# Attention quotients: reciprocals of all 512 columns of a group, in place of one column in 32 of turned squares

## The chip, the cores and the metric

The kernel runs on one core of one Trainium2 chip. The metric is the device time of one execution in microseconds. The engines are named as in the profile: PE (matmuls) with PEld (its weight loads), DVE (vector engine), ACT (scalar engine), POOL (GpSimd) and SP (which issues nearly all DMAs).

## The reference

A transformer block with adaptive layer norm. x is (8, 1024, 512) and the condition (8, 512), all fp32. The rows of the condition give six vectors per batch row (shift, gain and gate for attention and for the MLP).

```python
mod = jax.nn.silu(condition) @ Wada + bada
sh_a, sc_a, gt_a, sh_m, sc_m, gt_m = jnp.split(mod, 6, axis=1)
xm = (layernorm(x) * g1 + be1) * (1.0 + sc_a[:, None, :]) + sh_a[:, None, :]
x = x + gt_a[:, None, :] * attention(xm, Wqkv, Wproj, bproj)   # 16 heads of 32, causal softmax
xm = (layernorm(x) * g2 + be2) * (1.0 + sc_m[:, None, :]) + sh_m[:, None, :]
h = gelu(xm @ W1 + b1)                                          # 512 -> 2048, exact gelu
x = x + gt_m[:, None, :] * (h @ W2 + b2)
```

The place of interest is the division in the softmax: the weighed values of a head and a query are divided by the sum of that query's exponentials.

## The kernel before

**Blocks and groups.** The 8 x 1024 tokens are cut into 16 blocks of 512 tokens (`blocks`, `NB` = 16), two to a batch row. The 16 heads are cut into 4 groups of 4 (`NC` = 4, `HPG` = 4), since 4 heads of 32 channels fill 128 partitions. So there are 64 pairs of block n and group g. For each pair PE computes the scores twice: once row by row for the maxima (`scores`, tile `sc`, L1679), which DVE masks (L1691) and reduces (`mx`, L1694), and once transposed with the maxima subtracted (`weights_T`, tile `st`, L1758 and L1770). ACT exponentiates the latter into `pT` (L1782), POOL zeroes what lies above the diagonal (L1787) and adds the tiles of exponentials up (L1911). PE multiplies `pT` with the values into `po` (L1810). `sc` and `st` share one buffer of four PSUM banks.

**The end of a group.** `finish` has PE add up the exponentials over the keys by a product with a tile of ones (L1831). With 32 equal columns of ones for each head, each of a head's 32 partitions holds the same sum of a query: in the bank, a square of 32 partitions by 32 columns has 32 different sums, each repeated down a column. ACT copies the bank to `rec` (L1840) and `po` to `top` (L1843); both tiles have one buffer. Then DVE works in pieces. `gather(i)` transposes a quarter of `rec` in squares of 32x32 into `squares` (L1850), so that the sums of a square stand in one column, one to a partition, and takes the reciprocal of that one column in 32, four columns for a quarter (L1852, into `inverse`). `spread_out` transposes `inverse`, each column repeated 32 times, back over `rec` (L1857). The quotient, `top` times `rec`, is written into the block's query tile `qT`, which is free by then: by POOL (L1885) in 61 of the 64 groups, and by DVE in the last group of block 0 (`first_end`, L1874), the last but one of block 15 (L1882) and the last of all (L1866, in quarters).

**The projection and the rest.** `qT` then goes through Wproj (`project_out`; for the odd blocks, but the last, `project_quarters`), the second layer norm and the MLP. The linear layers use a Strassen-like scheme on halves of 256 (`strassen`, products of 16 matmuls on L217, evacuated by DVE at L208 and L194 or by ACT at L197 and L204). Block n's attention runs beside the linear layers of its neighbours, as `plan` lists them.

**What sets the order.** The order on each engine is written out when the program is built. `now` holds a clock for each engine; `note` adds the booked duration of an instruction to it and keeps when each tile is written and left. `step_aside`, `work` and `pace` choose with these clocks what PE does next (attention, or a step of the linear layers), and `sooner` and `either` choose the engine of some operations. DVE's work at the end of a group is handed to `add_job`; `run_jobs` puts jobs on DVE where its booked clock is not ahead of PE's, those of a block's last group ahead of others. For `first_end` and for the very last group the work is issued at once. So a booked duration that changes can move instructions of every engine. The bookings of the operations concerned are `160 + 1.05 * wide + 100` (`wide` = 128) for `gather`, `140 + 1.05 * m` (m = 512, or 128 at the very end) for `spread_out`, and 1285 for POOL's quotient.

**Loads.** SP issues the loads of weights into a ring of 8 buffers (`fetch`), of x, and of scratch copies in DRAM, in one queue. From block 2 on (two blocks at the end excepted) x is normalized, transposed in squares on DVE (L704), written to DRAM (L713) and read back turned (L718, `hat_a`), before gain and shift are applied (L775 on DVE, L781 on ACT) and sums for the products are formed (L791, L793). Two steps `gates` multiply the condition with parts of Wada (L524). In the opening `scores_by_heads` (L1649, L1666) takes a unit of scores head by head through the three banks of the linear layers where these are free.

Of the kernel before, what the change touches and what calls it, by code (L numbers as in the profile page):

```python
# [9 lines left out]
F32 = mybir.dt.float32  # L10
# [12 lines left out]
def kernel(  # L23
# [33 lines left out]
    nc = tc.nc  # L57
    B, T, D = x.shape
    HD = W1.shape[1]
    P = 128  # L60
    hd = D // H
    scale = float(hd) ** -0.5
    TB = 512
    NTT = TB // P
    NHALF = T // TB
    NC = D // P
# [15 lines left out]
    small = ctx.enter_context(tc.tile_pool(name="small", bufs=2))  # L82
# [22 lines left out]
    def due(reads=(), writes=()):  # L105
        t = 0.0
        for k in reads:
            t = max(t, written.get(k, 0.0))
        for k in writes:
            t = max(t, left.get(k, 0.0))  # L110
        return t

    def note(engine, ns, reads=(), writes=(), port=False):
        start = max(now[engine], due(reads, writes))
        if port:
            start = max([start] + [b for a, b in pool_spans if a <= start < b])
        end = start + ns
        now[engine] = end
        if engine == "POOL":
            pool_spans.append((start, end))  # L120
            del pool_spans[:-16]
        for k in reads:
            left[k] = max(left.get(k, 0.0), end + SYNC)
        for k in writes:
            written[k] = end + SYNC
        return end
# [9 lines left out]
    def note_pe(ns, form, reads=(), writes=()):  # L136
        now["PE"] = max(now["PE"], due(reads, writes))
        if shape[0] != form:
            shape[0] = form
            now["PE"] += SWITCH  # L140
        note("PE", ns, reads)
        spent[0] += ns
        for k in writes:
            written[k] = now["PE"] + PIPE

    def note_act(ns, func, reads=(), writes=()):
        if func is not None and table[0] != func:
            table[0] = func
            ns += TABLE
        note("ACT", ns, reads, writes)  # L150
# [31 lines left out]
    def lin_bank():  # L182
        i = min(
            (i for i in range(3) if not live[i]),
            key=lambda i: left.get(("l", i), 0.0),
        )
        live[i] = True
        return i
# [54 lines left out]
    def mlp_steps(n):  # L243
        return [("u", n, i) for i in range(NQ)] + [("d", n, part) for part in range(4)]
# [9 lines left out]
    for w in range(1, NB):  # L254
        n = w - 1
        m = mlp_steps(n)
# [29 lines left out]
    n = NB - 1  # L286
# [115 lines left out]
    Q = P // NTT  # L402
# [81 lines left out]
    def spread(o):  # L484
        return cols[:, o : o + NC].unsqueeze(2).to_broadcast([P, NC, B])

    def norm_columns(name, shift_at, gain_at, o_g, o_b):

        gain = const.tile([P, NC, B], F32, tag=f"gain{name}", name=f"gain{name}")
        shift = const.tile([P, NC, B], F32, tag=f"shift{name}", name=f"shift{name}")  # L490
        one_plus = small.tile([P, NC, B], F32, tag="onep", name=f"onep{name}", bufs=1)
        nc.vector.tensor_scalar(one_plus, modT[:, ts(gain_at, NC), :], 1.0, None, ALU.add)
        nc.vector.tensor_tensor(gain, one_plus, spread(o_g), ALU.mult)
        nc.vector.tensor_tensor(shift, one_plus, spread(o_b), ALU.mult)
        nc.vector.tensor_tensor(shift, shift, modT[:, ts(shift_at, NC), :], ALU.add)
        return gain, shift
# [60 lines left out]
    def add_job(job, reads, first=False):  # L557

        at = sum(1 for other in jobs if other[2]) if first else len(jobs)
        jobs.insert(at, (job, reads, first))  # L560

    def run_jobs(everything=False):
        while jobs and (
            everything or (now["DVE"] <= now["PE"] and due(jobs[0][1]) <= now["PE"])
        ):
            jobs.pop(0)[0]()
# [854 lines left out]
    def perform(step):  # L1421
        kind = step[0]
        if kind == "mod":
            yield from modulation(step[1])
        elif kind == "norm_columns_a":
            columns_of["a"] = norm_columns("a", 0, 1, O_G1, O_BE1)
        elif kind == "gates":
            yield from gates(step[1])
# [112 lines left out]
    def step_aside(reads, writes):  # L1541


        while threads():
            if linear_wait() == NEVER:
                hurry()
            own, other = wait_of((reads, writes)), linear_wait()
            if done_linear[0] < stream["due"]:
                if other > own + 100:
                    break  # L1550
            elif own <= max(other, 50):
                break
            work()
        while BANK in writes and bank_at() == NEVER:
            work()
        run_jobs()
        run_act_jobs()
        run_pool_jobs()
        run_preparation()
# [260 lines left out]
    def finish(n, g):  # L1820

        run_jobs(True)
        acc, slot = totals.pop((n, g))
        more = unadded if (n, g) == first_end else []
        step_aside([("acc", n, g), *(("p", slot) for *_, slot in more)], [BANK])
        bank = lin_bank()
        terms = [(0, TB, acc, slot)] + [(c0, w, pT, slot) for parts, pT, slot in more for _, c0, w, _ in parts]
        for i, (c0, w, term, held) in enumerate(terms):
            for j in range(HPG):
                r = slice(j * hd, (j + 1) * hd)  # L1830
                nc.tensor.matmul(  # L1831
                    banks[bank][r, TB - w :], ones, term[:, j, c0 : c0 + w],
                    start=i == 0, stop=i == len(terms) - 1, skip_group_check=True,
                )
            note_pe(2 * COLUMN * w, "columns", [("acc", n, g), ("p", held)], [("l", bank)])
        free_p.extend([slot, *(held for *_, held in more)])
        top = tmp.tile([P, TB], F32, tag="top", name=f"top_{n}_{g}", bufs=1)
        rec = tmp.tile([P, TB], F32, tag="rec", name=f"rec_{n}_{g}", bufs=1)
        kr = "rec"
        nc.scalar.copy(rec, banks[bank])  # L1840
        note_act(585, None, [("l", bank)], [kr])
        live[bank] = False
        nc.scalar.copy(top, outs.pop((n, g)))  # L1843
        note_act(585, None, ["po"], ["top"])
        part = TB // 4
        wide = TB // 4

        def gather(i):
            squares = small.tile([P, wide], F32, tag="squares", name=f"squares_{n}_{g}_{i}", bufs=1)
            nc.vector.transpose(squares, rec[:, ts(i, wide)])  # L1850
            some = inverse[:, ts(i, wide // Q)]
            nc.vector.reciprocal(some, squares.rearrange("p (a i) -> p a i", i=Q)[:, :, 0])  # L1852
            note("DVE", 160 + 1.05 * wide + 100, [kr], [kr])

        def spread_out(i=0, m=TB):
            some = inverse[:, i * m // Q : (i + 1) * m // Q].unsqueeze(2).to_broadcast([P, m // Q, Q])
            nc.vector.transpose(rec[:, ts(i, m)].rearrange("p (a i) -> p a i", i=Q), some)  # L1857
            note("DVE", 140 + 1.05 * m, [kr], [kr])

        inverse = small.tile([P, TB // Q], F32, tag="inverse", name=f"inverse_{n}_{g}", bufs=1)  # L1860
        if (n, g) == groups[-1]:
            for i in range(NTT):
                gather(i)
                spread_out(i, part)
                some = slice(i * part, (i + 1) * part)
                nc.vector.tensor_tensor(qTs[n][:, g, some], top[:, some], rec[:, some], ALU.mult)  # L1866
                note("DVE", 200, [kr, "top"], [("att", n, i)])
            return

        if (n, g) == first_end:  # L1870
            for i in range(4):
                gather(i)
            spread_out()
            nc.vector.tensor_tensor(qTs[n][:, g, :], top, rec, ALU.mult)  # L1874
            note("DVE", 700, [kr, "top"], [("att", n)], port=True)
            written["attended", n] = 0.0
            return

        def quotient():
            spread_out()  # L1880
            if n == NB - 1 and g == NC - 2:
                nc.vector.tensor_tensor(qTs[n][:, g, :], top, rec, ALU.mult)  # L1882
                note("DVE", 700, [kr, "top"], [("att", n)], port=True)
            else:
                nc.gpsimd.tensor_tensor(qTs[n][:, g, :], top, rec, ALU.mult)  # L1885
                note("POOL", 1285, [kr, "top"], [("att", n)])
            if g == NC - 1:
                written["attended", n] = 0.0

        for i in range(4):  # L1890
            add_job(lambda i=i: gather(i), [kr], g == NC - 1)
        add_job(quotient, [kr], g == NC - 1)

    shared = {}
# [194 lines left out]
```

## Time and profile before

| | |
|---|---|
| median of 3 runs | 3508.98 us (3507.87 to 3513.93) |
| the profiled execution | 3501.11 us, span 3499.4 us |
| granted TensorE clock | 0.998 of full speed, mean |
| busy: PE, DVE, POOL, ACT | 98%, 63%, 60%, 35% of the span |
| instructions: PE, DVE, POOL, ACT | 55101, 2808, 2255, 1272 |

Busy times add up over an engine's instructions. In rows of instructions the engine stands first, then what is written, what is read and the shapes. A time in square brackets is how long the engine was idle ahead of the row, and for whom. An fp32 matmul has two records in the trace.

### The profile page before, as it was taken

The numbers are of one execution on the slowest core, as the hardware profiler recorded it, in microseconds if no ns is written. First come the engines' busy times: TensorE is split into PE (matmuls) and PEld (weight loads), VectorE is DVE, ScalarE is ACT, GpSimd is POOL, SyncE is SP. The second block draws the span as 40 slices with busy tenths as digits, with TensorE's granted clock in tenths as the row PEclk, the third lists the DMA queues.
The fourth block names the chain that finished last, engine by engine and source line by source line (L and its number), as shares of the span: only waits on it lengthen the run. The fifth ranks groups of instructions, "written<-read, shape, count | busy, mean of one in ns | idle before, by whom it ended". The sixth has DMA issues, their size and how long they took to land. (4 is left out here: it accounts for less than half of the span.)

```text
span 3499.4 us, 122173 instructions
## 1 busy us (share of the span) xinstructions
PE 3441.3 (98%) x55101; PEld 1750.9 (50%) x55101; DVE 2203.8 (63%) x2808; ACT 1212.8 (35%) x1272; POOL 2113.7 (60%) x2255
## 2 busy tenths in 40 slices
PE   8999999999999999999999999999999999999999
PEld 4444455445544555445554455544555445554555
DVE  5775675565666566565666656665666656656573
ACT  2335333342343513335232442333423333323521
POOL 3667847667366663767627676375762857628640
PEclk9999999999999999999999999999999999999999
DMA  6763444535535455363554535545455454543344
GB/s 213 237 188 104 137 125 139 147 104 171 147 118 158 119 162 149 103 182 116 152 152 127 159 116 152 153 137 146 130 154 143 130 144 132 154 126 98 104 134 140
DMA packets 335580, 498.84 MB, mean 143 GB/s; under 512 B 27724, under 2 KB 184460, under 8 KB 331476
## 3 DMA queue, kind: packets, MB, share of 16 engines
q1 hardware_dynamic: 334944, 490.99, 47.8%
q8 instruction: 434, 7.11, 0.8%
q14 instruction: 86, 0.70, 0.1%
q10 hardware_dynamic: 116, 0.03, 0.0%
HBM read 432.13 MB, written 56.69 MB: 140 GB/s over the span
## 5 line engine op out<-in xcount | busy, mean ns | idle before, releaser
L1911 POOL TENSOR_TENSOR pT<-pT,pT 128x256 f32<-128x256 f32 (+3 forms) x1254 | 1224.7, 1012 | 238.9 <-PE po L1810 123.9
L1782 ACT ACTIVATE pT<-st 128x2048 f32<-128x2048 f32 x288 | 541.1, 1879 | 1017.5 <-PE st L1770 886.3
L217 PE MATMUL bank<-w,hT 128*32 128x256 f32 x14336 | 822.1, 380 | 0.0
L1694 DVE TENSOR_REDUCE mx<-sc 128x4 f32<-128x2048 f32 (+3 forms) x383 | 663.3, 1753 | 200.5 <-PE sc L1679 194.7
L217 PEld LDWEIGHTS bank<-w,hT 128*32 128x32 f32 x14336 | 448.0, 110 | 389.8 <-issue 109.7
L217 PE MATMUL bank<-xm_m,w 128*32 128x256 f32 x8192 | 497.4, 381 | 2.3 <-ACT p_u L197 1.0
L217 PE MATMUL bank<-t_m,w 128*32 128x256 f32 x6144 | 384.0, 380 | 2.5 <-DVE qT L208 1.4
L217 PEld LDWEIGHTS bank<-xm_m,w 128*32 128x32 f32 x8192 | 255.5, 110 | 227.3 <-issue 56.6
L1787 POOL TENSOR_SCALAR_AFFINE_SELECT pT<-pT 128x512 f32<-128x512 f32 x256 | 177.3, 710 | 313.7 <-ACT pT L1782 313.3
L1679 PE MATMUL sc<-kT,qT 32*128 32x512 f32 (+3 forms) x3064 | 328.0, 520 | 3.1 <-DVE mx L1694 1.8
L1691 DVE TENSOR_TENSOR sc<-sc,mask 128x1024 f32<-128x1024 f32 (+1 forms) x160 | 162.8, 1017 | 255.2 <-PE sc L1679 210.8
L1810 PE MATMUL po<-pT,v 128*32 128x512 f32 (+3 forms) x3048 | 301.7, 490 | 2.5 <-POOL pT L1787 2.3
L1770 PE MATMUL st<-qT,kT 32*128 32x512 f32 (+3 forms) x3072 | 302.7, 487 | 0.0
L217 PEld LDWEIGHTS bank<-t_m,w 128*32 128x32 f32 x6144 | 188.9, 110 | 178.8 <-issue 49.8
L217 PE MATMUL bank<-xm_a,w 128*32 128x256 f32 x3968 | 241.6, 380 | 2.4 <-ACT p_k L197 1.1
L1679 PEld LDWEIGHTS sc<-kT,qT 32*128 32x128 f32 x3064 | 129.2, 183 | 182.4 <-issue 82.4
L208 DVE TENSOR_TENSOR hT<-bank,u_u 128x512 f32<-128x512 f32 x186 | 126.0, 686 | 127.2 <-PE bank L217 126.5
L217 PE MATMUL bank<-t_a,w 128*32 128x256 f32 x2944 | 182.3, 380 | 1.4 <-ACT qT L204 0.9
L1885 POOL TENSOR_TENSOR qT<-top,rec 128x512 f32<-128x512 f32 x61 | 79.8, 1309 | 170.7 <-DVE rec L1857 167.8
L217 PE MATMUL bank<-w,qT 128*32 128x512 f32 (+1 forms) x1824 | 175.4, 515 | 3.7 <-DMA w<-in_L_cond_Wproj_dram 3.7
L1199 ACT ACTIVATE hT<-hT,cols 128x512 f32<-128x512 f32 x256 | 164.7, 711 | 40.7 <-DVE hT L208 27.4
L217 PEld LDWEIGHTS bank<-xm_a,w 128*32 128x32 f32 x3968 | 123.9, 110 | 101.3 <-issue 16.9
(262 smaller groups left out, 3657.1 us busy)
## 6 DMA issues: line engine op xcount, KB each, us to landing
w<-in_L_cond_W_dram SPq DMA_DIRECT2D x384, 256.0 KB
w<-kept_up_S SPq DMA_DIRECT2D x256, 256.0 KB
w<-kept_down_S SPq DMA_DIRECT2D x256, 256.0 KB
w<-kept_qkv_S SPq DMA_DIRECT2D x180, 256.0 KB
w<-in_L_cond_Wqkv_dram SPq DMA_DIRECT2D x147, 256.0 KB
hat_a<-in_x_dram SPq DMA_DIRECT2D x64, 256.0 KB
xr<-in_x_dram SPq DMA_DIRECT2D x32, 512.0 KB
out_dram<-xr SPq DMA_DIRECT2D x31, 512.0 KB
```

The costliest lines, as they stand in the source:

```text
L208: nc.vector.tensor_tensor(out, src, other, op)
L217: nc.tensor.matmul(ps[r, :], columns, rhs, start=start, stop=stop, skip_group_check=True)
L1199: nc.scalar.activation(hT[:, i, :], hT[:, i, :], AF.Gelu, bias=cols[:, O_B1 + f : O_B1 + f + 1])
L1679: nc.tensor.matmul(sc[:, j, c0 : c0 + w], qTs[n][r, gg, ts(qt, P)], keys_of(n, kh)[r, gg, :w], start=True, stop=True, skip_group_check=True,)
L1691: nc.vector.tensor_tensor(place, place, shape_of.to_broadcast(place.shape), ALU.add)
L1694: nc.vector.tensor_reduce(maxima[n, gg][:, kh, qt, :], sc[:, :, c0 : c0 + w], axis=AX.X, op=ALU.max)
L1770: nc.tensor.matmul(st[:, j, c0 : c0 + w], kT[r, gg, ts(k % NTT, P)], qT[r, gg, TB - w :], start=False, stop=True, skip_group_check=True,)
L1782: nc.scalar.activation(pT[:, :, :used], st[:, :, :used], AF.Exp, scale=scale)
L1787: nc.gpsimd.affine_select(diagonal, diagonal, pattern=[[0, HPG], [1, P]], compare_op=ALU.is_ge, fill=0.0, base=0, channel_multiplier=-1,)
L1810: nc.tensor.matmul(po[r, TB - w :], v[:, k % NTT, g * P + j * hd : g * P + (j + 1) * hd], pT[:, j, c0 : c0 + w], start=(k == 0), stop=last ...
L1885: nc.gpsimd.tensor_tensor(qTs[n][:, g, :], top, rec, ALU.mult)
L1911: nc.gpsimd.tensor_tensor(into, into, pT[:, j, c0 : c0 + w], ALU.add)
```

## The change

`gather`, `spread_out`, `squares` and `inverse` go. In their place `invert(i)` takes the reciprocal of a quarter of `rec`, 128 partitions by 128 columns, in place, in four calls for a group, each booked at 920 ns. Three calls are jobs of their own; the fourth stands ahead of the quotient, where `spread_out` stood. In the two groups whose work is issued at once the calls are issued at once too. The bookings of the quotients stay. A small tile of the layer norm's columns (`one_plus`) gets the pool's two buffers in place of one.

```diff
-        one_plus = small.tile([P, NC, B], F32, tag="onep", name=f"onep{name}", bufs=1)
+        one_plus = small.tile([P, NC, B], F32, tag="onep", name=f"onep{name}")
...
         part = TB // 4
-        wide = TB // 4
-
-        def gather(i):
-            squares = small.tile([P, wide], F32, tag="squares", name=f"squares_{n}_{g}_{i}", bufs=1)
-            nc.vector.transpose(squares, rec[:, ts(i, wide)])
-            some = inverse[:, ts(i, wide // Q)]
-            nc.vector.reciprocal(some, squares.rearrange("p (a i) -> p a i", i=Q)[:, :, 0])
-            note("DVE", 160 + 1.05 * wide + 100, [kr], [kr])
-
-        def spread_out(i=0, m=TB):
-            some = inverse[:, i * m // Q : (i + 1) * m // Q].unsqueeze(2).to_broadcast([P, m // Q, Q])
-            nc.vector.transpose(rec[:, ts(i, m)].rearrange("p (a i) -> p a i", i=Q), some)
-            note("DVE", 140 + 1.05 * m, [kr], [kr])
-
-        inverse = small.tile([P, TB // Q], F32, tag="inverse", name=f"inverse_{n}_{g}", bufs=1)
+
+        def invert(i):
+            some = rec[:, i * part : (i + 1) * part]
+            nc.vector.reciprocal(some, some)
+            note("DVE", 920, [kr], [kr])
+
         if (n, g) == groups[-1]:
             for i in range(NTT):
-                gather(i)
-                spread_out(i, part)
+                invert(i)
...
         if (n, g) == first_end:
-            for i in range(4):
-                gather(i)
-            spread_out()
+            for i in range(NTT):
+                invert(i)
...
         def quotient():
-            spread_out()
+            invert(3)
...
-        for i in range(4):
-            add_job(lambda i=i: gather(i), [kr], g == NC - 1)
+        for i in range(3):
+            add_job(lambda i=i: invert(i), [kr], g == NC - 1)
         add_job(quotient, [kr], g == NC - 1)
```

## The prediction

> **What bounds the kernel now.** I read the page's busy line first, then the stretches, then who waits for whom.
>
> ```profile
> span 3499.4 us, 122173 instructions
> PE 3441.3 (98%) x55101; PEld 1750.9 (50%) x55101; DVE 2203.8 (63%) x2808; ACT 1212.8 (35%) x1272; POOL 2113.7 (60%) x2255
> ```
> TensorE (PE) is busy for 3441.3 of 3499.4 us, so all that any edit outside the matmuls can win back is the 58.1 us in which it is idle. DVE, the engine that the change works on, is idle for 3499.4 - 2203.8 = 1295.6 us. The stretches show where the idle time of PE lies (columns: length, then PE, PEld, DVE, ACT, POOL busy, granted clock, DMA share, GB/s):
> ```profile
> 0.00:87.00 87.00, 72.41 (x1329) 43.48 (x1333) 51.22 (x79) 23.89 (x31) 27.55 (x40) 1.00 0.68 214
> 87.00:175.00 88.00, 81.28 (x1356) 41.62 (x1352) 65.66 (x101) 26.41 (x28) 61.40 (x78) 0.96 0.75 236
> 1400.00:1750.00 350.00, 348.27 (x5524) 175.87 (x5520) 216.78 (x272) 124.45 (x127) 243.43 (x252) 1.00 0.47 138
> ```
> The first 175 us, before the pipeline of blocks is full, hold 14.6 + 6.7 = 21.3 us of the idle time; a stretch in the middle loses 1.7 us in 350. So the interior hides nearly everything that DVE does, and the opening is where a later DVE can be seen. What PE waited for DVE, and whose weight loads did (us, times, longest; then us, times):
> ```profile
> PE st L1758 <- DVE mx L1694: 4.2, 6, 1.6
> PE bank L1649 <- DVE mx L1666: 2.2, 1, 2.2
> PE sc L1679 <- DVE mx L1694: 1.8, 3, 0.9
> ```
> ```profile
>   PEld L1758: 23.2, 48
>   PEld sc L1679: 13.2, 25
> ```
> The row maxima (L1694) are DVE's closest call: 48 + 25 = 73 weight loads found them not ready, but only 9 of those reached the matmuls, for 6.0 us. A DVE that is a little later at these places has little reserve.
>
> **The change: DVE's work.** These are the groups that go, with neighbours for the price of what comes (columns: busy us, mean ns of one, idle before it):
> ```profile
> L1850 DVE STREAM_TRANSPOSE squares<-rec 128x128 f32<-128x128 f32 x256 | 78.6, 307 | 60.0 <-ACT rec L1840 54.6
> L1852 DVE RECIPROCAL inverse<-squares 128x4 f32<-128x4 f32 x256 | 45.7, 178 | 8.8
> L1857 DVE STREAM_TRANSPOSE rec<-inverse 128x512 f32<-128x512 f32 x63 | 44.6, 708 | 2.9
> L1857 DVE STREAM_TRANSPOSE rec<-inverse 128x128 f32<-128x128 f32 x4 | 1.2, 312 | 0.1
> L686 DVE RECIPROCAL rstd_m<-rstd_m 128x1 f32<-128x1 f32 x4 | 0.6, 138 | 0.2 <-ACT rstd_m L681 0.2
> L208 DVE TENSOR_TENSOR kT<-bank,u_k 128x512 f32<-128x512 f32 x44 | 29.4, 686 | 12.8 <-PE bank L217 12.4
> L1694 DVE TENSOR_REDUCE mx<-sc 128x4 f32<-128x2048 f32 x191 | 437.3, 2290 | 197.2 <-PE sc L1679 194.7
> L1885 POOL TENSOR_TENSOR qT<-top,rec 128x512 f32<-128x512 f32 x61 | 79.8, 1309 | 170.7 <-DVE rec L1857 167.8
> ```
> Removed: 78.6 + 45.7 + 44.6 + 1.2 = 170.1 us in 579 instructions. Added: 256 reciprocals of 128x128, a shape that the trace does not have. From below: one pass of the same shape with a cheap operation takes 0.307 us (L1850). From above: going from one column to four costs 178 - 138 = 40 ns, 13.3 ns a column, and 138 + 127 x 13.3 = 1.83 us. I take 0.92 us, the duration that the changed code itself books for the call, because its other bookings stand on rows of this trace: it books 170 + 4.14 x 512 = 2290 ns for the reduction (row 2290) and 1285 ns for POOL's quotient (row 1309). So 256 x 0.92 = 235.5 us come in, DVE gains 65.4 us of busy time against 1295.6 idle, and its share goes from 63% to 65%. With the ends it is -91 us (0.307) or +298 us (1.83).
>
> The Trainium skill ("VectorE: DVE Perf Modes", section "First, the fixed hardware budget") says that a reciprocal runs as an iterative divide with a repeat count of 8, which speaks against spending it on 512 equal-valued columns. At that page's 0.96 GHz, eight cycles for each of 128 columns are an estimated 1.07 us before any fixed cost, between my value and my upper end; DVE would then gain about 104 us, still under a tenth of its idle time. The one-to-four-column rows above are steeper than that, and no run shows the wide shape yet.
>
> **One group's chain.** The last group of block 0, on DVE:
> ```profile
> 163.29 0.29 DVE L1850 STREAM_TRANSPOSE squares<-rec 128x128 f32<-128x128 f32 x1
> ...
> 163.83 0.31 DVE L1850 STREAM_TRANSPOSE squares<-rec 128x128 f32<-128x128 f32 x1
> ...
> 167.74 0.31 DVE L1850 STREAM_TRANSPOSE squares<-rec 128x128 f32<-128x128 f32 x1 [2.01 <-ACT rec L1840]
> ...
> 170.05 0.71 DVE L1857 STREAM_TRANSPOSE rec<-inverse 128x512 f32<-128x512 f32 x1
> 170.87 1.45 DVE L1874 TENSOR_TENSOR qT<-top,rec 128x512 f32<-128x512 f32 x1
> ```
> From 167.74 to 170.76 the chain takes 3.02 us. Four reciprocals with the gaps of 0.03 us seen here take 4 x 0.95 = 3.8 us, 0.8 us more for each of the 64 groups. The planner, which writes the order of all engines, booked 4 x 394 + 678 = 2.25 us before, so DVE ran 0.77 us behind its plan in every group; now it books 3.68 and runs 0.12 behind. The piece that may stand in front of an urgent reduction grows from 0.56 us (163.29 to 163.83 and the reciprocal's gap) to 0.95 us. POOL's quotient and, through the single buffer of rec, the next group's copy on ACT come later by the same 0.8 us; the rows of POOL above say that it waits 167.8 us for rec already and that only ACT waits for it, so this is cover, not path.
>
> **The opening.** The built program's order shows what the new bookings change: about 93% of PE's order stays, the matmuls are the same, the mode changes between them 1594 before and 1590 after. Two places in the first 180 us move.
> ```profile
> 142.38 1.14 PE L1679 MATMUL sc<-kT,qT 32*128 32x512 f32 x8 [0.84 <-ACT pT L1782]
> ...
> 146.57 1.21 PE L1649 MATMUL bank<-kT,qT 32*128 32x512 f32 x1 [2.19 <-DVE mx L1666]
> ...
> 150.70 1.08 PE L1810 MATMUL po<-pT,v 128*32 128x256 f32 x8
> 151.56 3.44 PE L524 MATMUL bank<-w,condT 128*8 128x256 f32 x11
> ...
> 156.23 1.09 PE L1770 MATMUL st<-qT,kT 32*128 32x384 f32 x16
> ...
> 161.03 1.05 PE L1810 MATMUL po<-pT,v 128*32 128x384 f32 x16
> 161.89 2.34 PE L1831 MATMUL bank<-pT,ones 128*32 128x512 f32 x32
> 164.16 1.14 PE L1679 MATMUL sc<-kT,qT 32*128 32x512 f32 x8
> ...
> 166.55 1.91 PE L217 MATMUL bank<-t_a,w 128*32 128x256 f32 x32
> ...
> 177.83 1.90 PE L217 MATMUL bank<-w,qT 128*32 128x512 f32 x16
> ```
> First, the unit computed head by head (L1649) becomes an ordinary one. It cost 2.19 us of idle time, and from 146.57 to 150.70 PE spent 4.1 us on little more than one attention unit (L1770, 1.09 us where it runs freely, and the rows ahead of it: about 1.5), so some 2.19 + 2.6 = 4.8 us are lost there. That goes. In its place stand gate matmuls (L524, 0.28 us each), a score unit, and three products of block 2's keys (1.9 us each, as at 166.55), which need that block's turned x:
> ```profile
> 150.68 1.00 DVE L775 TENSOR_SCALAR xm_a<-hat_a,gaina,shifta 128x512 f32<-128x512 f32 x2 [1.31 <-DMA b_out_m<-in_L_cond_b_dram]
> ...
> 152.67 1.51 ACT L781 ACTIVATE xm_a<-hat_a,shifta,gaina 128x512 f32<-128x512 f32 x2
> ...
> 154.21 0.69 DVE L793 TENSOR_TENSOR t_a<-xm_a 128x512 f32<-128x512 f32 x1 [1.80 <-ACT xm_a L781]
> ...
> 167.12 0.59 ACT L1840 COPY rec<-bank 128x512 f32<-128x512 f32 x1 [7.79 <-POOL qT L1885]
> ```
> x is there at 150.68 now. In the new order 1 MB of weight loads has moved behind it on SP's queue, 4.4 us at that stretch's 236 GB/s, so it lands between 146.3 and 150.7. PE gets there at about 148.5 (143.5 after the score unit, eight gate matmuls 2.2, a reduction of 2.3 on DVE before the next score unit of 1.1). The first product needs two passes on ACT (1.51 us), the second all four and two passes of 0.69 on DVE: x early, PE waits 0.5 us in all; x late, 4.9. No reason favours an end, so I take the middle, 2.7 us.
>
> Second, the projection of block 0 (L217 on qT) comes earlier. Before, 177.83 - 164.23 = 13.6 us of other matmuls stood between the sums (L1831) and it, and its input was ready at 172.32. In the new order only a score unit and two products stand there, 1.1 + 2 x 1.9 = 4.9 us. Counted from the score unit of the same opening that DVE must still reduce, PE arrives after one product, the weighing, the sums and those 4.9: 1.9 + 1.05 + 2.34 + 4.9 = 10.2 us. The chain to qT needs a reduction 2.3, an evacuation 0.7, a reciprocal 0.95, POOL's quotient of the group before 1.3 (its buffers must come free, as at 167.12), the copy 0.6, four reciprocals 3.8 and the product 1.45: 11.1 us. So PE waits 0.9 us where it did not, and every 0.1 us by which the reciprocal is dearer adds 0.5.
>
> **The interior.** In the new order a reciprocal stands directly ahead of a score unit's mask or reduction in 37 places. Each may delay it by 0.95 - 0.56 = 0.39 us, 14 us in all; of the late loads above 9 of 73 reached the matmuls, so 1.8 us.
>
> **The tail.** For the last group DVE is done 11 us before PE reads it, and its four pieces, 0.95 for reciprocals in place of some 0.9, add 0.2 us:
> ```profile
> 3360.06 0.30 DVE L1850 STREAM_TRANSPOSE squares<-rec 128x128 f32<-128x128 f32 x1
> ...
> 3365.74 0.29 DVE L1866 TENSOR_TENSOR qT<-top,rec 128x128 f32<-128x128 f32 x1
> ...
> 3376.97 14.09 PE L217 MATMUL bank<-w,qT 128*32 128x512 f32 x128
> ```
> Elsewhere in the new order some 20 us of matmuls or more stand between a block's last sums and its projection, as before. One more edit, a second buffer for a small tile used twice in the opening, costs nothing: its two uses lie far apart.
>
> **The sum.** -4.8 + 2.7 + 0.9 + 1.8 + 0 = +0.6 us. The profiled execution took 3501.11 us, 1.7 more than its span, and the median of the runs shown, 3508.98, lies 7.9 above it. So 3502 for a profiled run, and 3510 for the median. The three runs spread over 0.17%, so 0.2% (7 us) is about what can be told from no change.
>
> **Rivals.** *Reciprocals ahead of reductions (slower).* If the reserve at the maxima is below 0.39 us, the delay goes to PE whole: 14 us at the 37 places, 28 if all 73 late loads meet one, directly or behind a queue of two or three. For it: those 73 loads, and that the new order has three or four reciprocals in a row 36 times. Against: the planner now knows the long piece and puts it where it sees DVE idle. Time: 3509 + 14 = 3523; 30%.
> *A reciprocal of 1.83 us (slower).* A group then takes 7.4 us where 3.68 is booked, 3.7 behind plan instead of 0.77. If half of that extra 3 us reaches PE in 62 groups it is 93 us: 3602; 5%. Against: the bookings that agree with rows.
> *A truer plan (faster).* With DVE 0.12 instead of 0.77 us behind, the waits for the maxima go (6.0 us, nothing added), and x lands early (0.5): 3509 - 4.8 + 0.5 + 0.9 - 4 = 3501 to 3502, with 4 of the 6.0 gone; 13%. It decides from DVE's lag, not PE's work, being what the 73 loads met.
> *The change does not do what it says.* All 256 calls are in the built program; no chance.
>
> **How the numbers follow.** My own case (3510, within 3503 to 3518) has 52%, of which 4 points lie above 3516 and 1 below 3502; of the first rival's 30, 3 lie below 3516, and of the third's 13, 1 lies above 3502. So faster 0.13, same 0.51, slower 0.36. The range from 3501 to 3527 takes in the first rival's 14 us; it leaves out the 1.83 us reciprocal, most of the case with all 73 loads, and the best of the faster ones.
>
> **What would show it.** Reciprocals of 0.92 us, DVE at about 2269 us busy, a PE wait of 1 us at block 0's projection and 1 to 5 at the first products on block 2's x, no L1649, and PE's idle time outside the opening unchanged within a few us. I am wrong if the reciprocal is not between 0.8 and 1.1 us, if the opening as a whole moves by more than 5 us, or if waits on the maxima in the interior grow by more than 10 us.

## The result, and the profile after

The changed kernel takes 3509.69 us (median of 22 runs, 3504.51 to 3516.52) against 3503.52 us for the kernel before beside it (22 runs, 3500.9 to 3513.93): a ratio of 1.0015, with an interval of 1.0009 to 1.0022. So it is 5 to 6 us slower (5.3 by the ratio, 6.2 by the medians), inside the 0.2% that the prediction called no change. The forecast of 3510 us and the case "same" hold. But the interval leaves out 1: the loss is real, and it doesn't come from where the prediction put it.

The profiled execution took 3514.26 us. Its busy line:
```profile
span 3512.5 us, 121861 instructions
PE 3448.6 (98%) x55101; PEld 1751.6 (50%) x55101; DVE 2251.2 (64%) x2470; ACT 1216.4 (35%) x1280; POOL 2111.2 (60%) x2258
```
DVE gained 2251.2 - 2203.8 = 47.4 us. The matmuls are the same 55101, but PE's busy time rose by 7.3 us: they ran more slowly. The mean granted clock is 0.996, where it was 0.998, so the clock cost about 0.004 x 3512.5 = 14 us in this execution and 7 in the one before. PE's idle time went from 58.1 to 3512.5 - 3448.6 = 63.9 us. The 7.3 us of busy time and the 5.8 us of idle time are the 13.1 us between the two spans. That is more than the 5 to 6 us of the medians: executions of one kernel scatter by some 12 us, and this one lies 4.6 us above its kernel's median. The new group, in the view of groups that keeps shapes apart:
```profile
L1849 DVE RECIPROCAL rec<-rec 128x128 f32<-128x128 f32 x256 | 225.9, 920 | 55.2 <-ACT rec L1840 55.2
```
One takes 920 ns. Back to back they overlap a little, so that 256 keep DVE busy for 225.9 us (0.88 each). The stretches, by the same columns as in the prediction:
```profile
0.00:87.00 87.00, 73.69 (x1325) 42.80 (x1329) 51.83 (x78) 23.29 (x30) 27.46 (x40) 1.00 0.68 214
87.00:175.00 88.00, 84.11 (x1464) 42.79 (x1452) 68.74 (x79) 28.49 (x31) 64.81 (x82) 1.00 0.86 266
1400.00:1750.00 350.00, 348.68 (x5552) 175.57 (x5548) 226.76 (x248) 125.45 (x128) 233.58 (x241) 1.00 0.47 139
```
In the first 175 us PE is idle for 17.2 us where it was 21.3; the stretch in the middle loses 1.3 us in 350 where it lost 1.7. Neither holds the loss. Who waits for the row maxima (weight loads first, then matmuls):
```profile
  PEld L1758: 24.9, 48
  PEld sc L1679: 11.6, 23
  PE st L1758: 9.3, 6
  PE sc L1679: 3.0, 6
```
71 weight loads came too early, where 73 did before. Matmuls waited 12 times for 12.3 us, before 9 times for 6.0. Most of this growth is one wait early on, 4.59 us ahead of the row that starts at 217.97; it was 0.90 us before. It takes back what the first 175 us had won. Up to the start of the next group's sums (251.86 us before, 251.67 after) the two kernels have the same number of matmuls behind them, and PE was idle for 22.65 us before and 22.74 after:
```profile
0.00:251.86 251.86, 229.21 (x3717) 118.29 (x3721) 172.73 (x239) 72.94 (x79) 149.88 (x180) 0.99 0.70 217
0.00:251.67 251.67, 228.93 (x3717) 116.53 (x3721) 174.77 (x211) 75.50 (x83) 149.02 (x181) 0.99 0.70 217
```

### The profile page after: what moved, and what is told of

It is laid out like the page before. It is cut to its first block, busy times and chain, and to the rows that moved or that the text cites. A ratio compares the mean times of both kernels' runs of the same rounds, so it can differ in the third digit from the quotient of the medians.

```text
span 3512.5 us, 121861 instructions
## 1 busy us (share of the span) xinstructions
PE 3448.6 (98%) x55101; PEld 1751.6 (50%) x55101; DVE 2251.2 (64%) x2470; ACT 1216.4 (35%) x1280; POOL 2111.2 (60%) x2258
## 4 chain that ended last, share of the span: by engine, by line
PE 83%; DMA 5%; POOL 4%; DVE 4%; ACT 2%; issue 1%; SPq 1%; ACTq 0%; DVEq 0%; POOLq 0%
PE bank L217 58%; PE sc L1679 8%; PE st L1770 6%; PE po L1810 6%; POOL pT L1900 3%; PE st L1758 2%; PE bank L1831 2%; DVE mx L1694 1%; DMA hat_m<-held_m 1%; DMA hat_a<-held_a 1%; ACT pT L1782 1%; DMA held_a<-xm_a 1%; DVE sc L1691 1%; ACT xm_m L781 0%; DMA held_m<-xm_m 0%
## 5 line engine op out<-in xcount | busy, mean ns | idle before, releaser
L1849 DVE RECIPROCAL rec<-rec 128x128 f32<-128x128 f32 x256 | 225.9, 920 | 55.2 <-ACT rec L1840 55.2
```

The costliest lines, as they stand in the source:

```text
L1849: nc.vector.reciprocal(some, some)
```

## The experiments

**1 to 4: the work or the order.** The change does two things at once: DVE gets other instructions, and the new bookings make the planner write another order for every engine. My theory after the result was that the order costs and the work doesn't; the rival was that the longer reciprocals delay the maxima. Two kernels do one part each; two more keep the new order and take work away or add it. (`new_order_old_work` and `new_order_double_work` also give `one_plus` its single buffer back.)

`old_order_new_work` has the reciprocals of 128 columns, but in the slots and with the bookings of the old gather calls, so that the order on PE, ACT, POOL and SP is that of the kernel before.
```diff
-            nc.vector.transpose(squares, rec[:, ts(i, wide)]) ...
+            some = rec[:, ts(i, wide)]
+            nc.vector.reciprocal(some, some)
             note("DVE", 160 + 1.05 * wide + 100, [kr], [kr])
         def spread_out(i=0, m=TB):
-            nc.vector.transpose(...)
             note("DVE", 140 + 1.05 * m, [kr], [kr])
```


> The reciprocals of 128 columns run in the slots of the transposes, with the old bookings, so that PE, ACT, POOL and SP have the order of before instruction by instruction; DVE does 47 us more. Theory 'order' (the 6 us, ratio 1.0015, come from the order that the new bookings wrote, above all from one wait of 4.6 us for the maxima at 218 us and from what the clock does after waits of about 2 us): ratio to before 1.0000, within 0.0007; the wait at 218 us stays at 0.9 us. Theory 'work' (they come from DVE's longer chain in each group): ratio 1.0010 to 1.0020, and waits on the maxima (L1694) of 8 us or more in place of 6.0.

`new_order_old_work` has the transposes and the reciprocals of one column in 32, in the slots and with the bookings of the changed kernel.
```diff
         def invert(i):
-            nc.vector.reciprocal(some, some)
+            nc.vector.transpose(squares, rec[:, ts(i, part)])
+            nc.vector.reciprocal(some, squares.rearrange("p (a i) -> p a i", i=Q)[:, :, 0])
+            if m == part or i == 3:
+                nc.vector.transpose(rec[:, ts(k, m)].rearrange("p (a i) -> p a i", i=Q), some)
             note("DVE", 920, [kr], [kr])
```


> Transposes and the reciprocal of one column in 32 run in the slots of the four new calls, with the new bookings of 920 ns, so that PE, ACT, POOL and SP have the order of the changed kernel; DVE does 47 us less than it. Theory 'order': ratio to before 1.0010 to 1.0020, and the wait at 218 us stays between 4 and 5 us. Theory 'work': ratio 1.0000, within 0.0007.

`new_order_quarter_work` is the changed kernel with three of four reciprocals left out (three quarters of the quotients are products with the sums).
```diff
-            nc.vector.reciprocal(some, some)
+            if i == 3:
+                nc.vector.reciprocal(some, some)
```


> The changed kernel with three of the four reciprocals of a group left out (three quarters of the quotients are then products with the sums), at unchanged bookings: the order of the changed kernel, DVE busy some 165 us less. Theory 'order': ratio to before 1.0005 to 1.0015, since what DVE saves was hidden. Theory 'work': the ratio falls below that of before, 0.995 to 0.999.

`new_order_double_work` takes each reciprocal twice, first into a scratch tile.
```diff
+            again = small.tile([P, part], F32, tag="again", name=f"again_{n}_{g}_{i}", bufs=1)
+            nc.vector.reciprocal(again, some)
             nc.vector.reciprocal(some, some)
```


> The changed kernel with every reciprocal taken twice, first into a scratch tile that nothing reads, at unchanged bookings: the order of the changed kernel, DVE busy some 220 us more (about 2470), a group's chain 3.4 us longer. Theory 'order': DVE's idle time hides most of it, ratio to before 1.0015 to 1.0040. Theory 'work': if 47 us of DVE cost 6, 220 cost some 28 more, ratio 1.008 to 1.012.

| order | work | DVE busy, us | median, us | ratio (interval) |
|---|---|---|---|---|
| old | old (before) | 2203.8 | 3503.52 | 1 |
| old | new | 2251.6 | 3503.23 | 0.9999 (0.9989 to 1.0008) |
| new | old | 2194.8 | 3509.50 | 1.0019 (1.0010 to 1.0028) |
| new | a quarter | 2096.7 | 3509.70 | 1.0020 (1.0011 to 1.0029) |
| new | new (after) | 2251.2 | 3509.69 | 1.0015 (1.0009 to 1.0022) |
| new | double | 2469.8 | 3561.36 | 1.0161 (1.0147 to 1.0175) |

The order costs, the work doesn't. With the old order the new work is free; in the new order DVE may do 155 us less (2251.2 to 2096.7) and nothing comes back. The doubled kernel missed what both theories expected of it: DVE's time is free at +47 us and not at +266, where the 219 us beyond the changed kernel cost 52 us. There waits for the maxima reach PE:
```profile
  PEld L1758: 33.8, 52
  PEld sc L1679: 19.5, 24
  PE st L1758: 16.8, 20
  PE sc L1679: 10.4, 6
```
26 matmuls wait for 27.2 us (12 for 12.3 in the changed kernel), though little more than the same number of loads (76) come early. That is 15 of the 37 us by which PE's idle time grew (63.9 to 100.9 us); by the mean clock, 0.993, some 11 us more went to it, and the other waits lie elsewhere. So there is a reserve, larger than the changed kernel needs and smaller than the doubled one does; how large it is at the maxima alone is not measured.

**5 and 6: which blocks.** The bookings and slots of the changed kernel in block 0 alone, and in all blocks but block 0; the reciprocals are wide in both.
```diff
+        booked_new = n == 0      # new_order_block0_only;  n > 0 in new_order_from_block1
...
-            note("DVE", 920, [kr], [kr])
+            note("DVE", 920 if booked_new else 160 + 1.05 * wide + 100, [kr], [kr])
```


> The reciprocals of 128 columns everywhere, booked at 920 ns in block 0 and with the old bookings (and slots) from block 1 on: PE has the changed kernel's order up to about 400 us, then nearly that of before. Theory 'opening' (the loss of 6 us arises where the two orders differ most, in the first 400 us, with the wait for the maxima at 218 us and the half clock after it): ratio to before 1.0010 to 1.0020. Theory 'later' (it arises from small differences in blocks 3 to 8 and at the end of block 13, after which the marks of the two traces stay apart): ratio 0.9995 to 1.0007.

> The counterpart: old bookings and slots in block 0, 920 ns from block 1 on, reciprocals of 128 columns everywhere. PE has the order of before up to about 200 us and then nearly that of the changed kernel. Theory 'opening': ratio 0.9995 to 1.0007. Theory 'later': ratio 1.0010 to 1.0020.

Block 0 alone gives 1.0002 (0.9992 to 1.0011), the others 1.0009 (1.0000 to 1.0017), which lies between what the two theories expected. The opening, on which the prediction spent most of its working, is worth nothing that can be told from zero. The point estimates put what there is behind it, but the two intervals overlap, so these two kernels alone don't settle it.

**Where it is.** I set the same marks in two traces: the start of each group's sums. At the last group's sums the two traces lie 12.2 us apart. From the last group of block 7 to the first of block 9 is the largest loss that the changed kernel shares with `new_order_old_work` and `new_order_quarter_work`. The marks in the kernel before and in the changed one:
```profile
1665.28 1.04 PE L1831 MATMUL bank<-pT,ones 128*32 128x512 f32 x8
...
1914.63 1.38 PE L1831 MATMUL bank<-pT,ones 128*32 128x512 f32 x8
```
```profile
1670.93 1.04 PE L1831 MATMUL bank<-pT,ones 128*32 128x512 f32 x8
...
1923.79 1.38 PE L1831 MATMUL bank<-pT,ones 128*32 128x512 f32 x8
```
249.35 us before, 252.86 after: 3.5 us in this stretch. The other kernels with this order here lose as much, those without it don't (against the kernel before): `new_order_old_work` 4.0, `new_order_quarter_work` 3.0, `new_order_from_block1` 5.1; `old_order_new_work` 0.1, `new_order_block0_only` 0.7. Inside it, DVE's timeline of the kernel before:
```profile
1766.79 0.69 DVE L208 TENSOR_TENSOR u_q<-bank,p_q 128x512 f32<-128x512 f32 x1 [3.68 <-PE bank L217]
1770.18 0.69 DVE L208 TENSOR_TENSOR u_q<-bank,u_q 128x512 f32<-128x512 f32 x1 [2.71 <-PE bank L217]
1772.45 0.55 DVE L775 TENSOR_SCALAR xm_m<-hat_m,gainm,shiftm 128x512 f32<-128x512 f32 x1 [1.58 <-DMA hat_m<-held_m]
```
and of the changed kernel, on DVE and then on PE:
```profile
1773.29 0.77 DVE L775 TENSOR_SCALAR xm_m<-hat_m,gainm,shiftm 128x512 f32<-128x512 f32 x1 [2.01 <-DMA w<-in_L_cond_W_dram]
...
1776.25 1.66 DVE L167 TENSOR_TENSOR t_m<-t_m,xm_m 128x512 f32<-128x512 f32 x1
1777.83 1.21 DVE L167 TENSOR_TENSOR t_m<-xm_m,t_m 128x512 f32<-128x512 f32 x1
1778.96 0.68 DVE L208 TENSOR_TENSOR u_q<-bank,p_q 128x512 f32<-128x512 f32 x1
```
```profile
1776.01 1.93 PE L217 MATMUL bank<-t_a,w 128*32 128x256 f32 x32 [0.32 <-ACT qT L197]
1779.69 0.64 PE L217 MATMUL bank<-xm_m,w 128*32 128x256 f32 x8 [1.75 <-DVE u_q L208]
```
Before, DVE empties the two banks of queries (`u_q`) and then turns to the input of block 7's MLP (L775 and the sums behind it). In the new order that input stands ahead of both evacuations in DVE's queue. Its first instruction waits for a transfer until 1773.29 (the row names a weight load as what ended the wait; in the kernel before it is the load of `hat_m`, which the instruction reads), and everything behind it waits along. PE, which needs one of those banks, stands still for 1.75 us. What follows is in the windows of the changed kernel (the clock is the third number from the end):
```profile
1778.00:1780.00 2.00, 0.31 (x8) 0.16 (x8) 1.90 (x3) 0.00 (x0) 2.00 (x3) 1.00 0.47 117
1780.00:1782.00 2.00, 1.84 (x32) 0.88 (x28) 1.12 (x2) 0.00 (x0) 0.99 (x2) 0.82 0.04 15
1782.00:1784.00 2.00, 2.00 (x24) 0.94 (x20) 0.55 (x1) 0.00 (x0) 0.00 (x0) 0.50 0.03 8
1784.00:1786.00 2.00, 2.00 (x36) 1.21 (x32) 0.24 (x2) 0.00 (x0) 0.00 (x0) 0.83 0.46 131
```
The granted clock falls to one half for 3.4 us: 2 x (0.18 + 0.50 + 0.17) = 1.7 us of lost clock, as much as the wait itself. The whole stretch, with the same matmuls, in the kernel before and in the changed one:
```profile
1665.28:1914.63 249.35, 247.21 (x4044) 129.37 (x4038) 162.18 (x213) 74.40 (x82) 142.03 (x155) 1.00 0.48 139
1670.93:1923.79 252.86, 249.59 (x4045) 128.62 (x4040) 172.03 (x189) 75.47 (x84) 139.99 (x152) 0.99 0.47 137
```
PE's idle time grew from 2.14 to 3.27 us only, since the kernel before has waits of its own here (1.15 us for a weight load, 0.70 us for ACT). With the 1.7 us of clock that is 2.8 of the 3.5 us; the rest is not assigned. It is one place of many, so it had to be tested by itself.

**7: that place alone.** `one_place_mended` is the changed kernel, with one booked time moved: the planner is told that the turned x of block 7's MLP comes 5 us later, so it puts that input behind the evacuations.
```diff
             note_dma(1250, [("held", key)], [("turned", key)])
+        if key == "m7":
+            written["turned", key] += 5000
```


> The changed kernel with one more booking altered: the turned rows of block 7's MLP input are booked to land 5 us later. With it DVE's queue at about 1780 us has the two evacuations u_q ahead of the five operations on that input, as in the order of before, instead of behind them; only some 30 instructions on each engine stand otherwise than in the changed kernel. Theory 'place' (more than half of the 6 us arise there: five runs with the evacuations behind show a wait of 1.7 to 2.2 us on u_q, a dip of the clock behind it, and 3 to 5 us between the sums of the last group of block 7 and those of the first of block 9 beyond the order of before; runs with the old order there show 0.6 to 1.2): that difference falls to 1.3 us or less, the wait on u_q and the dip at 1780 us are gone, ratio to before 1.0002 to 1.0010. Theory 'given back' (PE waits for something else in the same stretch): the difference stays above 2 us, ratio 1.0012 to 1.0020.

0.9998 (0.9989 to 1.0006): nothing of the loss is left that can be told from zero, even a little less than the theory of the place expected. DVE's timeline and the clock there:
```profile
1769.93 0.69 DVE L208 TENSOR_TENSOR u_q<-bank,p_q 128x512 f32<-128x512 f32 x1 [1.09 <-PE bank L217]
1773.33 0.69 DVE L208 TENSOR_TENSOR u_q<-bank,u_q 128x512 f32<-128x512 f32 x1 [2.71 <-PE bank L217]
1773.94 2.89 DVE L777 TENSOR_SCALAR xm_m<-hat_m,gainm,shiftm 128x512 f32<-128x512 f32 x1
```
```profile
1778.00:1780.00 2.00, 2.00 (x44) 1.18 (x38) 1.97 (x4) 0.00 (x0) 1.50 (x1) 1.00 0.43 124
```
The evacuations come first, PE has no idle time there and the clock stays at 1.00. The same two marks stand at 1668.70 and 1916.83:
```profile
1668.70 1.04 PE L1833 MATMUL bank<-pT,ones 128*32 128x512 f32 x8
...
1916.83 1.39 PE L1833 MATMUL bank<-pT,ones 128*32 128x512 f32 x8
```
```profile
1668.70:1916.83 248.13, 247.13 (x4045) 128.07 (x4039) 170.95 (x187) 76.08 (x85) 141.05 (x154) 1.00 0.48 140
```
248.13 us, 4.7 less than in the changed kernel, with 1.00 us of idle time in the whole stretch. The edit also moves later instructions, and both ratios have intervals of about 0.1%, so the remainder between these 4.7 us and the 6 us between the two ratios isn't assigned. Another loss that both kernels have is not what parts them: from the first sums of block 3 to those of block 4 the changed kernel loses 3.1 us against the kernel before and `one_place_mended` 3.0. And the place accounts for the loss of this kernel, not for that of every order: `new_order_from_block1` loses 5.1 us there and has 1.0009 in all, and `booked_560` (below) loses 0.15 us there and has 1.0023.

**8 to 11: other bookings.** If a smaller booking gave a better plan, the order could be kept good by choosing the number. Four kernels change it alone.
```diff
-            note("DVE", 920, [kr], [kr])
+            note("DVE", 700, [kr], [kr])      # and 560, 850, 1000
```


> The changed kernel with the call booked at 700 ns, 150 below the pace at which it runs. Theory 'a truer plan is a faster one': slower than the run at 850, ratio to before 1.0010 or more. Theory 'the less DVE is booked, the better the order': at or below the run at 850, 0.9990 to 1.0007. Theory 'lottery': 0.998 to 1.004 without a trend.

> The changed kernel with the call booked at 850 ns, the pace at which four calls in a row run in its trace (3.39 us for four), in place of 920. Theory 'a truer plan is a faster one': ratio to before at or below 1.0010, faster than the changed kernel (1.0015). Theory 'lottery' (each booking writes another order, and orders scatter by some 0.1 to 0.2% without a trend in the booking): anything between 0.998 and 1.004.

> The changed kernel with the call booked at 1000 ns, 150 more than the pace at which it runs. Theory 'a truer plan is a faster one': slower than the changed kernel, ratio to before 1.0020 or more. Theory 'lottery': anything between 0.998 and 1.004, on either side of the run at 850.

> The changed kernel with the call booked at 560 ns, so that a group is booked at 2.24 us, as before the change, though in four slots in place of five. Theory 'a truer plan is a faster one': ratio to before 1.0015 or more. Theory 'the less DVE is booked, the better the order': 0.9990 to 1.0005, as the old order with the new work (0.9999). Theory 'lottery': 0.998 to 1.004 without a trend.

Booked at 560, 700, 850, 920 and 1000 ns the ratios are 1.0023 (1.0014 to 1.0032), 1.0000 (0.9991 to 1.0009), 1.0007 (0.9998 to 1.0015), 1.0015 and 1.0019 (1.0010 to 1.0027). That less is better falls with 560, which is slower than 700. The three largest bookings would fit a slope, and so would chance. The stretch from block 7 to block 9 costs 4.0 us at 1000, 0.9 at 850, 0.7 at 700 and 0.15 at 560, so the loss at 560 must be elsewhere; I have not found it. Four calls of 560 are 2.24 us a group, as much as the old slots book (2.25), and those gave 0.9999: for about the same booked time two slot patterns lie 0.24% apart. This speaks for a lottery of orders rather than a best booking, but five points don't settle it.

**12: an attempt at a version faster than both.** `old_order_tail_filled` is `old_order_new_work` with the last projection started as soon as its input is there, and half of the MLP step beside it kept back to fill PE's wait for the last layer norm.
```diff
         if kind == "beside":
-            return pieces_of(step[1])
+            own = pieces_of(step[1])
+            return own[:NQ] + [(Wproj, 0, k) for k in range(NC)] + own[NQ:]
...
-        return sides + ([main] if main[0] is not None else [])
+        own = [main] if main[0] is not None else []
+        return own + sides[::-1] if closing[0] else sides + own
```


> The reciprocals of 128 columns with the old bookings and slots, and one change more, at the end: the last projection is started as soon as its input is there, with its weights loaded between the two halves of the MLP step that ran ahead of it, and the second half of that step is left for the time in which the last layer norm keeps PE waiting (2.63 + 0.33 + 0.3 us idle in the traces, followed by 4 to 7 us at half clock). The matmuls are the same. Theory 'a wait costs more than itself' (after some 2 us without matmuls PE runs at half clock for 3.4 to 7 us): ratio to before 0.9975 to 0.9986 (5 to 9 us), no dip of the clock near the end of block 15's projection. Theory 'a wait costs itself' (the dips come at that time whatever PE does): 0.9988 to 0.9995 (2 to 4 us), and the dip stays.

0.9996 (0.9986 to 1.0006): less than expected, and not to be told from no change. The place itself did what it should. `old_order_new_work`, PE's row at the wait and the window:
```profile
3393.90 0.48 PE L771 MATMUL bank<-ident,hat_m 128*128 128x128 f32 x1 [2.63 <-ACT hat_m L691]
```
```profile
3380.00:3400.00 20.00, 16.79 (x144) 7.18 (x136) 12.66 (x28) 6.39 (x11) 0.74 (x1) 0.83 0.28 93
```
and the same window of `old_order_tail_filled`:
```profile
3380.00:3400.00 20.00, 20.00 (x276) 9.53 (x272) 15.29 (x31) 5.61 (x10) 3.78 (x3) 1.00 0.37 114
```
PE is not idle and the clock stays whole. From the last sums to the end of the span it took 146.2 us in place of 150.6. But this execution reached its last sums 8.5 us later than the kernel before (3357.8 against 3349.35), although PE's order is the same up to there. A gain of 4 us in 3500 is at the edge of what eleven runs show.

## Why the prediction was right or wrong

**Right: a change inside 0.2%, and why the work is free.** DVE's idle time hides the reciprocals; with the order held, 47.8 us more of DVE cost -0.01% (-0.11 to +0.08%).

**Right: the price of the reciprocal.** 0.92 us was taken and 920 ns measured. The ends, 0.307 and 1.83, are out, and with the upper one the rival of 3602 us. The doubled kernel measures that rival's mechanism: its 219 us more of DVE cost 52 us, where the rival, with 233 us more, allowed 93; so it was also priced nearly twice too high. The Trainium skill ("VectorE: DVE Perf Modes", section "First, the fixed hardware budget") led to an estimate of 1.07 us by its repeat count of 8; measured are 0.92 us for one and 3.39 us for four in a row, 0.85 each, so here the measurement is lower.

**Off by a quarter: what DVE gains.** Forecast 65.4 us (2269 busy), measured 47.4 (2251.2). The calls overlap (225.9 us and not 235.5), and 15 other instructions left DVE, while ACT and POOL gained 11 (1272 to 1280, 2255 to 2258).

**The opening.** The net forecast was -4.8 + 2.7 + 0.9 = -1.2 us. PE's rows of the changed kernel at the three places:
```profile
146.27 1.14 PE L1679 MATMUL sc<-kT,qT 32*128 32x512 f32 x8 [0.22 <-DVE mx L1694]
...
149.02 1.93 PE L217 MATMUL bank<-xm_a,w 128*32 128x256 f32 x32 [0.45 <-DMA w<-in_L_cond_Wqkv_dram]
...
171.88 2.76 PE L217 MATMUL bank<-w,qT 128*32 128x512 f32 x24
```
L1649 is gone, as forecast. But of the 4.8 us set down for it, 2.6 were read from a stretch in which the clock was halved, and no term was made of that: in the kernel before the granted clock is 0.50 from 146.54 on, for 6.8 us. `old_order_new_work` has the same order and a like wait, its clock stays at 1.00, and from 147.59 to 149.71 it takes 2.1 us for what took 4.1:
```profile
146.54:149.95 3.41, 3.38 (x14) 1.56 (x14) 1.86 (x3) 0.00 (x0) 2.67 (x4) 0.50 1.07 246
```
```profile
147.59 0.69 PE L1649 MATMUL bank<-kT,qT 32*128 32x512 f32 x1 [2.49 <-DVE mx L1666]
...
149.71 0.64 PE L1810 MATMUL po<-pT,v 128*32 128x256 f32 x8
```
So the unit cost its wait and some 0.6 us, and the other 2 us belonged to that execution. The x of block 2 came at its early end: ACT began to read it at 147.06, and PE lost 0.45 us ahead of its products (its row names a weight load), so the middle of 2.7 us was too much. The projection of block 0 shows no wait where 0.9 was forecast. The reciprocals of its last group ran from 168.33 to 171.72, and the quotient from 171.83; PE began at 171.88, with the parts of the query tile that were ready. These two terms were too high and the gain of the first place was too, and the wait of 4.59 us ahead of 217.97 was not foreseen. Together they are near zero (22.65 us of idle time up to the next sums, then 22.74), and block 0's new order alone gave 1.0002: no change, as the small net sum says, but not by its terms.

**The step that failed: the interior.** It put 1.8 us on reciprocals that stand ahead of reductions, 37 places times 0.39 us times 9 in 73. That mechanism doesn't act: the late loads are 71 in place of 73, and leaving three quarters of the reciprocals out wins nothing. The measured 5 to 6 us in its place come from something for which the sum had no term. "About 93% of PE's order stays" was read as if a moved order cost nothing beyond the opening; one swap in DVE's queue, of instructions that the change doesn't touch, stopped PE for 1.75 us and halved the clock after it. One of the prediction's own signs says the same: PE's idle time outside the opening, expected unchanged within a few us, is 63.9 - 17.2 = 46.7 us in the trace, where it was 58.1 - 21.3 = 36.8.

**Luck: the number.** The forecast was a change of +0.6 us, set on 3508.98 us, the median of three runs. The median of 22 runs of the kernel before is 3503.52 us, 5.5 lower. That the start was 5.5 us too high and the change 5 to 6 us too small cancel, which is why 3510 stands beside 3509.69. The change itself was forecast too small, within the 0.2% that was allowed for.

**The rivals.** Reciprocals ahead of reductions at 14 us: fallen, with quarter and double work. The truer plan: not seen; bookings nearer the measured time (850, 920) are not better than 700, and waits for the maxima grew from 6.0 to 12.3 us. This growth is the order's too: the wait ahead of the row at 217.97 is 4.59 us in the changed kernel and 3.38 in `new_order_old_work` and in `new_order_quarter_work`, which have less DVE work at group ends. It cost nothing that the median shows once the one place was mended.

## What to carry to other kernels

Where a planner writes the order, an edit to one engine's instruction has two prices: its work, and the other order that its booking brings. Hold one and change the other (old slots with new work, new slots with old work) before you explain a fraction of a per cent. To find such a loss, set the same marks in both traces, look for the stretch where their distance jumps, and see there which queue has an instruction that waits for a transfer ahead of one that the matmuls need. Read the granted clock beside every row from which a cost is taken: a stretch at half clock can belong to that execution alone.

## What was not expected of the hardware

A wait of PE can cost twice: with an idle time of some 2 us the granted clock often fell to 0.50 for a few us. In the changed kernel it did after waits of 1.75 us (the windows at 1778 to 1786 above), 2.27, 2.43, 2.63 and 2.75 us, and during the 4.59 us ahead of 217.97:
```profile
218.00:220.00 2.00, 2.00 (x12) 0.66 (x11) 2.00 (x3) 0.00 (x0) 2.00 (x3) 0.50 0.08 25
```
But not always. In the kernel before, 2.10 us of idle time ahead of 2984.2 left it whole, and in `new_order_quarter_work` so did a wait of 2.20 us at the very place of block 7's MLP, where the expectation of `one_place_mended` counted a dip.

The traces show most of what decides. Within each of the 14 profiled executions, the spells of half clock begin at whole multiples of 3.413 us from one another and last one, two or three such steps (the last spell runs into the program's end). From one execution to the next this grid lies elsewhere against the program. What counts in the main is the idle time inside one step of the grid. In the changed kernel the wait of 1.75 us and the 0.16 us behind it fall into one step, which leaves PE busy for 1.51 of 3.41 us, and the next step is at half clock:
```profile
1777.87:1781.28 3.41, 1.51 (x28) 0.70 (x28) 3.15 (x5) 0.00 (x0) 3.12 (x4) 1.00 0.31 81
1781.28:1784.69 3.41, 3.41 (x40) 1.71 (x34) 0.69 (x1) 0.00 (x0) 0.00 (x0) 0.50 0.06 12
```
In the kernel before the border between two steps cuts the wait of 2.10 us, and neither step is idle for more than 1.2 us:
```profile
2979.60:2983.01 3.41, 2.48 (x48) 1.23 (x40) 2.77 (x5) 1.78 (x3) 1.06 (x2) 1.00 0.75 243
2983.01:2986.42 3.41, 2.24 (x44) 1.38 (x48) 2.01 (x3) 0.82 (x2) 3.33 (x3) 1.00 0.28 77
```
From 35 us on and up to the last 4 us of the 14 traces, all 48 steps at full clock with 2.09 us or more of idle time were followed by a step at half clock, none with 1.66 us or less, and 10 of the 18 between, where something else must decide too. So whether a wait of 2 us halves the clock depends on where the grid happens to lie in that execution. This is part of the scatter: of the 8.5 us between the two executions at their last sums, 5.1 are half clock (spells of 17.1 us in all, against 6.8).

The Trainium skill ("TensorE: Matmul & The Clock Gate", section "Part 1: The HAM clock gate (the "warmup" mystery)") tells of a half rate after an idle window of about 3.4 us, with windows that run free of the program. The half rate, the length of the steps and their running free agree with these traces. Read as a window without any work, the rule doesn't: 1.9 of 3.4 us of idle time sufficed, and the measurement decides.
